# Layer 3 of a four-layer convolution stack: shifts from 8 on computed on TensorE as four 32-column tiles

## The chip, the cores and the metric

The kernel runs on one core of one Trainium2 chip. The metric is the device time of one execution in microseconds (us), given as the median over several runs. A profile of one execution comes beside it; its times are counted from the first instruction of that execution.

## The reference

Four layers work on `x`, an image of 4 batches, 32 rows, 32 columns and 16 channels in fp32. Each adds to `x` a function of `x` after a group norm. Layers 0 to 2 mix pixels with large dense tensors; they are not touched here. Layer 3 is a two-dimensional causal convolution with a filter given by its transfer function, written in the reference with Fourier transforms:

```python
def _L3_conv_ref(x, h0, numerators, denumerator):
    a = jnp.pad(denumerator, ((0, 0), (0, 0), (1, 0), (1, 0)), constant_values=1.0)
    b = jnp.pad(numerators, ((0, 0), (0, 0), (0, 0), (1, 0), (1, 0)), constant_values=0.0)
    H_truncated = jnp.fft.rfft2(b, s=(l1, l2)) / jnp.fft.rfft2(a, s=(l1, l2))
    h_truncated = jnp.fft.irfft2(H_truncated, s=(l1, l2))
    H = jnp.fft.rfft2(h_truncated, s=(2 * l1, 2 * l2))
    H_full = h0 + H[0]
    X = jnp.fft.rfft2(x, s=(2 * l1, 2 * l2), axes=(-3, -2))
    Y = jnp.einsum('...hwi,ijhw->...hwj', X, H_full)
    return jnp.fft.irfft2(Y, s=(2 * l1, 2 * l2), axes=(-3, -2))[..., :l1, :l2, :]
...
x = x + _L3_conv_ref(_gn(x), L3_conv_h0, L3_conv_numerators, L3_conv_denumerator)
```

What counts for this case: an output pixel in column w takes input pixels of columns w, w-1, ..., 0 only. An input that lies d columns to the left meets the filter's column d. The number d is called the shift; it runs from 0 to 31, and an output column w has no work for a shift above w.

## The kernel before

Nearly all of the time goes to layers 0 to 2 (`conv_layer`, matmuls of L336 and the multiply-and-sum of L344). The filter of layer 3 (its impulse response) is worked out beside layer 0 and left in DRAM as `hd`. Layer 3 itself is the last stretch of the program, and nothing of any other layer stands beside it.

The group norm of layer 3 leaves its result in `y3`, with partitions (8 image rows x 16 channels), then four row groups `cc`, then 31 zero columns followed by the 32 image columns, then the batch. A slice of `y3` that begins at column 31-d is the image shifted by d to the right, with zeros where it runs out of the image. This slice is the stationary operand (`lhsT`) of a matmul: 32 columns x 4 batches = 128 output partitions. So output partition n holds column n/4 of the image, and each quarter of 32 partitions ("block" in the change) holds eight image columns.

The moving operand (`rhs`) comes from a Toeplitz tile `t`, which `load_toeplitz(k)` builds from `hd` for four shifts, 4k to 4k+3 (`TQ` is 4; k runs from 0 to 7). It is made of eight DMAs (L501), four issued on SP and four on ACT, one for each group of 16 partitions. Each DMA carries 160 KB in runs of 640 bytes, so one tile is 1.31 MB. The pool `tp` holds three such tiles. The first three are loaded during layer 2 (`toeplitz`, stepped by `conv_layer`). The load of tile k+2 is written in the program at the beginning of step k, and it goes to the buffer that step k-1 has read; SP and ACT wait for TensorE's semaphore before they issue it.

The program is written with a manual schedule: each engine runs its instructions in the order in which they are written.

The loop over k, q and cc issues 8 x 4 x 4 = 128 matmuls at L564, all into one PSUM bank `po`. The width of a matmul's output falls with cc (16 channels x 32, 24, 16 and 8 rows: 512, 384, 256 and 128 columns). The trace has two matmul records and two weight loads for each fp32 matmul. After the loop VectorE adds `po` to `xo` (L571; `xo` is `x` transposed, L553), and SP stores `xo` (L572).

Of the kernel before, what the change touches and what calls it, by code (L numbers as in the profile page):

```python
# [32 lines left out]
ALU = mybir.AluOpType  # L33
# [4 lines left out]
P = 128  # L38
B, C, S = 4, 16, 32
# [8 lines left out]
PITCH = 40  # L48
HLEN = 8 + S * PITCH
TQ = 4  # L50
# [3 lines left out]
def conv_stack_kernel(ctx, tc, x, M, W, G, den, num, h0, cst, dft, one, idp, idq, out):  # L54
    nc = tc.nc
# [14 lines left out]
    def pair_psum():  # L70
        return ps.tile([P, 2, 512], F32, tag="pt", name="pt")

    def small_psum():
        return pair_psum()[:, 0, :]
# [420 lines left out]
    def load_toeplitz(k):  # L495

        t = tp.tile([P, C, TQ * PITCH], F32, tag="t", name="t")
        hv = hd.rearrange("(j i) t -> i j t", j=C)
        for p in range(8):
            at = 8 + k * TQ * PITCH - p  # L500
            (nc.sync, nc.scalar)[p % 2].dma_start(  # L501
                out=t[p * C : (p + 1) * C], in_=hv[:, :, at : at + TQ * PITCH]
            )
        return t
# [17 lines left out]
    y3 = const.tile([P, 4, 31 + S, B], F32, name="y3")  # L522
# [11 lines left out]
    tp = ctx.enter_context(tc.tile_pool(name="tp", bufs=3))  # L534
    ts = []

    def toeplitz():
        for k in range(3):
            ts.append(load_toeplitz(k))
            yield  # L540

    xs = conv_layer(2, xs, norm3, toeplitz())
    drain()

# [7 lines left out]
    xo = work.tile([P, S, C], F32, tag="xo", name="xo")  # L552
    nc.scalar.copy(xo, px.rearrange("n (r j) -> n r j", j=C))  # L553

    po = small_psum()
    pov = po.rearrange("n (j r) -> n j r", j=C)
    for k in range(S // TQ):
        if k and k + 2 < S // TQ:
            ts.append(load_toeplitz(k + 2))
        t = ts[k]  # L560
        for q in range(TQ):
            dq = k * TQ + q
            for cc in range(4):
                nc.tensor.matmul(  # L564
                    pov[:, :, 8 * cc :],
                    lhsT=y3[:, cc, 31 - dq : 31 - dq + S, :].rearrange("p q b -> p (q b)"),
                    rhs=t[:, :, q * PITCH : q * PITCH + S - 8 * cc],
                    start=(dq == 0 and cc == 0),
                    stop=(dq == S - 1 and cc == 3),
                )  # L570
    nc.vector.tensor_tensor(xo, xo, pov.rearrange("n j r -> n r j"), ALU.add)  # L571
    nc.sync.dma_start(out=out, in_=xo)  # L572


# [81 lines left out]
```

## Time and profile before

| | |
|---|---|
| median of 3 runs | 3216.66 us (3215.99 to 3217.17) |
| profiled execution | 3216.64 us, of which 3214.8 us lie between its first and last instruction |
| layer 3's matmuls (L564) | from 3140.5 to 3210.9 us |
| 5 loads of `t` after the first three | issued from 3150.5 to 3191.3 us |
| final add (L571), store (L572) | from 3211.0 us, 0.69 us; issued at 3211.7 us |

The profile names the engines PE (TensorE's matmuls), PEld (its weight loads), DVE (VectorE), ACT (ScalarE), POOL (GpSimd) and SP (SyncE). A name with a q behind it is that engine's instruction queue. A line such as `L564 PE MATMUL pt<-t,y 128*128 128x512 f32` is a group of instructions: the source line, the engine, the operation, the tile written and the tiles read, the part of the array in use (rows * columns), and the shape of the result. `PEclk` is the granted share of TensorE's full clock. `DMA share` is the mean busy share of the core's 16 DMA engines; it can exceed 1, since an engine can have two packets under way at once.

### The profile page before, as it was taken

How to read it: one execution, taken by the hardware profiler on the slowest of the kernel's cores; microseconds unless marked ns; L12 is line 12 of the kernel's file. 1: busy time of each engine (PE TensorE's matmuls, PEld its weight loads, DVE VectorE, ACT ScalarE, POOL GpSimd, SP SyncE). 2: the span in 40 equal slices, each digit the busy share in tenths (PEclk: the TensorE clock that was granted, in tenths of full speed). 3: DMA queues.
4: the chain of work that ended last, by engine and by line, in shares of the span. 5: the costliest groups of instructions: out<-in, count | busy, mean ns of one | idle time of the engine just before them, and what ended most of it. 6: DMA issues, size and time to landing. Idle time of an engine off the chain costs nothing.

```text
span 3214.8 us, 38408 instructions
## 1 busy us (share of the span) xinstructions
PE 3148.2 (98%) x15852; PEld 1678.7 (52%) x15852; DVE 2054.8 (64%) x3294; ACT 75.7 (2%) x98; POOL 171.9 (5%) x124
## 2 busy tenths in 40 slices
PE   6999999999999999999999999999989999999998
PEld 3545566666666544444544445454444444444445
DVE  4666765666666766666666666766656666666660
ACT  0000000000000000000000000000000000000000
POOL 0002310000000000000000000000000000000000
PEclk9999999999999999999999999999999999999999
DMA  6544344343333554333433343365473343333306
GB/s 148 156 115 116 88 109 94 86 103 88 88 98 90 107 154 118 99 89 88 99 96 86 86 105 87 80 143 144 99 127 89 98 99 89 87 99 92 86 1 85
DMA packets 106383, 322.18 MB, mean 100 GB/s; under 512 B 29214, under 2 KB 59360, under 8 KB 81632
## 3 DMA queue, kind: packets, MB, share of 16 engines
q1 hardware_dynamic: 68608, 302.69, 39.2%
q10 hardware_dynamic: 37600, 17.04, 3.4%
q8 instruction: 124, 2.03, 0.3%
q14 instruction: 51, 0.42, 0.1%
HBM read 313.01 MB, written 6.68 MB: 99 GB/s over the span
## 4 chain that ended last, share of the span: by engine, by line
PE 94%; DMA 4%; DVE 1%; ACTq 0%; issue 0%; SPq 0%; POOL 0%; ACT 0%; DVEq 0%; POOLq 0%
PE pt L336 90%; PE pt L564 2%; DMA t<-hd 1%; DMA img<-y 1%; DMA im<-img 1%; PE pt L199 1%; DMA td<-s 1%; DMA v<-td 0%; DMA fd<-ft 0%; DVE junk L344 0%; DMA h0s<-in_h_dram 0%; PE pt L470 0%; ACTq L223 0%; PE pt L387 0%; POOL hs L452 0%
## 5 line engine op out<-in xcount | busy, mean ns | idle before, releaser
L344 DVE SCALAR_TENSOR_TENSOR junk<-pt,w 128x1024 f32<-128x1024 f32 x1536 | 1880.8, 1224 | 1031.7 <-PE pt L336 1017.4
L336 PE MATMUL pt<-im,ga 64*128 64x512 f32 x6144 | 1834.4, 592 | 38.0 <-DMA im<-img 20.5
L336 PE MATMUL pt<-im,gb 64*128 64x512 f32 x6144 | 1824.4, 589 | 0.9 <-DMA im<-img 0.9
L336 PE MATMUL pt<-im,gn 64*128 64x512 f32 x3072 | 1487.7, 807 | 1.9 <-DMA im<-img 1.9
L336 PEld LDWEIGHTS pt<-im,gb 64*128 64x128 f32 x6144 | 706.5, 186 | 737.7 <-issue 705.0
L336 PEld LDWEIGHTS pt<-im,ga 64*128 64x128 f32 x6144 | 708.6, 188 | 422.8 <-DVE junk L344 246.6
L336 PEld LDWEIGHTS pt<-im,gn 64*128 64x128 f32 x3072 | 355.3, 186 | 295.4 <-issue 290.2
L266 POOL TENSOR_TENSOR ga<-ga,cs 128x1024 f32<-128x1024 f32 x48 | 113.4, 2362 | 2215.5 <-DMA ga<-in_G_dram 2153.5
L273 DVE TENSOR_TENSOR gn<-g,gn 32x1024 fp32r<-32x1024 f32 x96 | 118.0, 1229 | 34.3 <-ACT gn L270 32.3
L344 DVE DVE_READ_ACCUMULATOR junk<-pt,w 128x1 f32 x1536 | 127.3, 83 | 0.0
L270 ACT CAST gn<-g 128x1024 fp32r<-128x1024 f32 x48 | 50.2, 1047 | 2318.7 <-DMA g<-in_G_dram 2020.4
L564 PE MATMUL pt<-t,y 128*128 128x512 f32 (+3 forms) x256 | 70.4, 438 | 0.0
L564 PEld LDWEIGHTS pt<-t,y 128*128 128x128 f32 x256 | 44.2, 193 | 26.2 <-issue 16.2
L571 DVE TENSOR_TENSOR xo<-xo,pt 128x512 f32<-128x512 f32 x1 | 0.7, 689 | 70.8 <-PE pt L564 70.8
L199 PE MATMUL pt<-mt,yt 128*64 128x512 f32 x96 | 21.9, 598 | 0.0
L231 POOL TENSOR_TENSOR xr<-x,xf 128x512 f32<-128x512 f32 x3 | 3.8, 1271 | 294.5 <-DMA xf<-fd 294.5
L470 PE MATMUL pt<-v,inv 64*128 64x512 f32 x16 | 8.6, 656 | 7.5 <-DMA v<-td 7.5
L199 PEld LDWEIGHTS pt<-mt,yt 128*64 128x64 f32 x96 | 6.4, 136 | 13.7 <-issue 9.4
L147 POOL COPY e<-y 32x612 f32<-32x612 f32 x6 | 4.2, 693 | 171.7 <-DVE y L146 171.7
L104 PE MATMUL pt<-s,cs 128*128 128x2 f32 x16 | 3.3, 276 | 9.7 <-DVE s L101 9.7
L408 POOL TENSOR_TENSOR H<-H,d 128x256 f32<-128x256 f32 (+1 forms) x10 | 8.2, 825 | 66.6 <-DVE d L413 66.3
L408 POOL TENSOR_TENSOR t<-s 128x256 f32<-128x256 f32 (+1 forms) x15 | 11.3, 754 | 0.0
(57 smaller groups left out, 141.0 us busy)
## 6 DMA issues: line engine op xcount, KB each, us to landing
w<-in_W_dram SPq DMA_DIRECT2D x192, 1024.0 KB
ga<-in_G_dram SPq DMA_DIRECT2D x96, 256.0 KB
gb<-in_G_dram SPq DMA_DIRECT2D x96, 256.0 KB
g<-in_G_dram SPq DMA_DIRECT2D x48, 512.0 KB
mt<-in_M_dram SPq DMA_DIRECT2D x24, 512.0 KB
t<-hd SPq DMA_DIRECT2D x32, 160.0 KB
t<-hd ACTq DMA_DIRECT2D x32, 160.0 KB
im<-img ACTq DMA_DIRECT2D x72, 67.5 KB
```

The lines of the kernel that those rows point to most:

```text
L104: nc.tensor.matmul(pm[:, :2], lhsT=avg, rhs=s, start=True, stop=True)
L147: nc.gpsimd.tensor_copy(ye[a][96:, :, :, 1:, :], ys[a][96:, :, :, :3, :])
L199: nc.tensor.matmul(pf[64 * h : 64 * h + 64], lhsT=yt[:, 4 * part + k].rearrange("k b c -> k (b c)"), rhs=mts[k][:, h, :], start=(k == 0), ...
L231: nc.gpsimd.tensor_tensor(xr, xt, xf, ALU.add)
L266: nc.gpsimd.tensor_tensor(gv, gv, mid.unsqueeze(1).to_broadcast([P, GC * 8, C]), ALU.subtract)
L270: nc.scalar.copy(gn, g9)
L273: nc.vector.tensor_tensor(lo, g9[r : r + 32], lo.bitcast(F32), ALU.subtract)
L336: nc.tensor.matmul(pt[:, half, :], lhsT=w[rows, blk % GC, :], rhs=im[rows, :, b % 2, :, :S], start=n == 0, stop=n == 2,)
L344: nc.vector.scalar_tensor_tensor(junk, pt.rearrange("p h m -> p (h m)"), 0.0, wt, ALU.min, ALU.mult, accum_out=acc[b // 2][:, b % 2, blk : ...
L408: mul = lambda o, u, w: nc.gpsimd.tensor_tensor(o, u, w, ALU.mult)
L470: nc.tensor.matmul(pq[:, h, :], lhsT=inv[two], rhs=v[two, bass.ts(part, 8)].rearrange("g p m -> g (p m)"), start=True, stop=True,)
L564: nc.tensor.matmul(pov[:, :, 8 * cc :], lhsT=y3[:, cc, 31 - dq : 31 - dq + S, :].rearrange("p q b -> p (q b)"), rhs=t[:, :, q * PITCH : q ...
```

## The change

Shifts 0 to 7 (k of 0 and 1) are computed as before. For shifts from 8 on, TensorE's array is used as four tiles of 128 rows x 32 columns. Each tile takes one quarter of the output (a block, eight image columns) and one shift of its own, with its own stationary and moving operand. Pairs of block and shift in which every stationary value is zero are left out: for shifts 8 to 15 three blocks are left, for 16 to 23 two, for 24 to 31 one. The list `slots` packs the pairs that remain in fours: 3 slots for each k of 2 and 3, 2 for 4 and 5, and 1 for 6 and 7. A slot is run for each of the four `cc`.

Where a block is computed in the tile of its own PSUM quarter, it adds to `po`. In the other cases the tile's quarter differs from the block's; the sum goes to another bank (`other`), and VectorE adds it to the right quarter of `xo` later (five adds of 32 partitions, L566). A second pair of PSUM banks is taken for that.

The order of the k is no longer 0 to 7 but 1, 7, 6, 5, 4, 3, 2, 0, and the loads follow this order. After the change the matmul is at L591, the final add at L606 and the store at L607.

In the built program the 128 matmuls become 32 matmuls of 128 output partitions and 192 of 32. The number and the size of the DMAs on SP and on ACT are the same, and so is all that stands ahead of layer 3 except for which k the first three loads take.

```diff
+    order = [1, 7, 6, 5, 4, 3, 2, 0]
+
     def toeplitz():
-        for k in range(3):
+        for k in order[:3]:
             ts.append(load_toeplitz(k))
             yield
...
-    po = small_psum()
-    pov = po.rearrange("n (j r) -> n j r", j=C)
-    for k in range(S // TQ):
-        if k and k + 2 < S // TQ:
-            ts.append(load_toeplitz(k + 2))
-        t = ts[k]
-        for q in range(TQ):
-            dq = k * TQ + q
+    banks = [pair_psum(), pair_psum()]
+    po, other = banks[0][:, 0], {1: banks[0][:, 1], 2: banks[1][:, 0], 3: banks[1][:, 1]}
+    def add(block, tile, bank):
+        out = xo[32 * block : 32 * block + 32]
+        src = bank[32 * tile : 32 * tile + 32].rearrange("n (j r) -> n r j", j=C)
+        nc.vector.tensor_tensor(out, out, src, ALU.add)
+
+    slots = [
+        [[(None, None, q)] for q in range(TQ)],
+        [[(0, i + 1, 3)] + [(t, t, i) for t in range(1, 4)] for i in range(3)],
+        [[(0, 2, 2 + i), (1, 3, 2 + i), (2, 2, i), (3, 3, i)] for i in range(2)],
+        [[(t, 3, t) for t in range(4)]],
+    ]
+    group = lambda tile, block: (tile, block) if tile != block else None
+    every = [group(*m[:2]) for k in order for slot in slots[k // 2] for _ in range(4) for m in slot]
+    done = 0
+    for n, k in enumerate(order):
+        if n and n + 2 < len(order):
+            ts.append(load_toeplitz(order[n + 2]))
+        for slot in slots[k // 2]:
             for cc in range(4):
-                nc.tensor.matmul(
-                    pov[:, :, 8 * cc :],
-                    lhsT=y3[:, cc, 31 - dq : 31 - dq + S, :].rearrange("p q b -> p (q b)"),
-                    rhs=t[:, :, q * PITCH : q * PITCH + S - 8 * cc],
-                    start=(dq == 0 and cc == 0),
-                    stop=(dq == S - 1 and cc == 3),
-                )
-    nc.vector.tensor_tensor(xo, xo, pov.rearrange("n j r -> n r j"), ALU.add)
+                for tile, block, q in slot:
+                    at = 31 - TQ * k - q
+                    if tile is None:
+                        bank, cols, width = po, slice(0, P), S
+                    else:
+                        bank = po if tile == block else other[block]
+                        cols, width = slice(32 * tile, 32 * tile + 32), 8
+                        at += 8 * block
+                    nc.tensor.matmul(
+                        bank[cols].rearrange("n (j r) -> n j r", j=C)[:, :, 8 * cc :],
+                        lhsT=y3[:, cc, at : at + width, :].rearrange("p q b -> p (q b)"),
+                        rhs=ts[n][:, :, q * PITCH : q * PITCH + S - 8 * cc],
+                        start=group(tile, block) not in every[:done],
+                        stop=group(tile, block) not in every[done + 1 :],
+                    )
+                    done += 1
+        if k == 6:
+            add(3, 2, other[3])
+        elif k == 4:
+            add(3, 1, other[3])
+        elif k == 2:
+            for block in range(1, 4):
+                add(block, 0, other[block])
+    nc.vector.tensor_tensor(xo, xo, po.rearrange("n (j r) -> n r j", j=C), ALU.add)
     nc.sync.dma_start(out=out, in_=xo)
```

## The prediction

> **What bounds the kernel now.** I read the page first, then the chain of waits for the last 75 us, then the groups of that stretch by shape, then its windows with the DMA share, and last the DMA queues. On the page TensorE is busy for 98% of the span, and layer 3's matmuls are 70.4 us of it:
>
> ```profile
> PE 3148.2 (98%) x15852; PEld 1678.7 (52%) x15852; DVE 2054.8 (64%) x3294; ACT 75.7 (2%) x98; POOL 171.9 (5%) x124
> L564 PE MATMUL pt<-t,y 128*128 128x512 f32 (+3 forms) x256 | 70.4, 438 | 0.0
> L571 DVE TENSOR_TENSOR xo<-xo,pt 128x512 f32<-128x512 f32 x1 | 0.7, 689 | 70.8 <-PE pt L564 70.8
> ```
>
> The chain of waits of the last stretch (start, length, what) says that these matmuls alone set the end; no wait stands between them:
>
> ```profile
> 3140.71 70.21 PE pt L564 x256
> 3210.92 0.03 issue
> 3210.95 0.02 DVEq L571
> 3210.97 0.04 issue
> 3211.01 0.69 DVE xo L571
> ```
>
> So a faster matmul loop ought to help one for one, until the next thing is late. What is next is seen in the windows, whose last two columns are DMA share and GB/s:
>
> ```profile
> 3140.00:3150.50 10.50, 10.50 (x37) 6.55 (x36) 0.23 (x1) 0.58 (x1) 0.00 (x0) 0.86 0.01 2
> 3150.50:3160.80 10.30, 10.30 (x38) 6.35 (x38) 0.00 (x0) 0.00 (x0) 0.00 (x0) 1.00 0.97 134
> 3160.80:3170.40 9.60, 9.60 (x38) 6.12 (x37) 0.00 (x0) 0.00 (x0) 0.00 (x0) 1.00 1.16 156
> 3170.40:3179.90 9.50, 9.50 (x36) 5.86 (x35) 0.00 (x0) 0.00 (x0) 0.00 (x0) 1.00 1.25 135
> 3179.90:3191.30 11.40, 11.40 (x45) 7.38 (x44) 0.00 (x0) 0.00 (x0) 0.00 (x0) 1.00 1.24 139
> 3191.30:3199.70 8.40, 8.40 (x32) 5.25 (x31) 0.00 (x0) 0.00 (x0) 0.00 (x0) 1.00 0.94 99
> 3199.70:3211.00 11.30, 11.21 (x43) 7.01 (x42) 0.00 (x0) 0.00 (x0) 0.00 (x0) 1.00 0.00 0
> ```
>
> I cut the windows where, by the trace's semaphore updates, the last DMA of each of the five late loads of `t` lands: 3160.83, 3170.41, 3179.93, 3191.25 and 3199.70. From the first load to the last the DMA engines have no free time. The DMA view of 3150 to 3200 us confirms it, in 40 slices and for both queues:
>
> ```profile
> DMA  0699999689999999999999999999999999999910
> q1 hardware_dynamic: 5440, 3.28, 56.0%
> q10 hardware_dynamic: 5440, 3.28, 53.8%
> t<-hd SPq DMA_DIRECT2D x20, 160.0 KB
> ```
>
> The stretch thus has two limits that nearly touch. The last step of matmuls (four shifts, 8.63 us) starts at about 3210.9 - 8.6 = 3202.3; its tile has landed at 3199.7. There are 2.6 us between the two.
>
> **What the skill says.** (1) "TensorEngine Tiling (Array Packing)", Key Properties: column tiles load weights and multiply independently of one another, and a change of the tiling mode drains the array. The trace agrees for two tiles: layer 0's first term uses 128*64 tiles with two moving operands,
>
> ```profile
> 180.47 3.65 PE L199 MATMUL pt<-mt,yt 128*64 128x512 f32 x16
> 3144.70 1.49 PEld L564 LDWEIGHTS pt<-t,y 128*128 128x128 f32 x7 [0.24 <-issue]
> 3146.86 1.49 PEld L564 LDWEIGHTS pt<-t,y 128*128 128x128 f32 x7 [0.24 <-issue]
> ```
>
> 16 records in 3.65 us. In layer 3 a record of this width follows the last one after 0.43 us, so one after another they would take 6.9. The two weight-load lines give the period of one shift (two records each of 512, 384, 256 and 128 columns): 2.16 us. (2) "TensorE: Matmul & The Clock Gate", Part 3, measured 2.38x for three column tiles and 10.6x for 16 tiles of 32x32. No run here shows four yet. (3) The same page, Part 1: an idle window of some 3.4 us halves TensorE's clock. The trace agrees: the granted clock is 0.50 from 3136.0 to 3142.9, after little work. (4) "Trainium Kernel Development and Optimization", Key Constraints: DMAs issued by SP and ACT share the same 16 engines. The trace agrees: 56.0% + 53.8% of them.
>
> **The change, part by part.**
>
> *Matmuls.* Before: 32 shifts x 2.16 = 69.1 us, and 1.3 us more for the half clock at the start. After: 8 full shifts, and 3+3+2+2+1+1 = 12 slots of four tiles. A slot has the widths of a shift. With four tiles side by side it costs 2.16 us, so 20 x 2.16 = 43.2 us: 25.9 us of matmul time go. The slot's price is the unknown. Below 2.16 it cannot go, since each tile streams its own 1280 columns twice. Above: 4.3 if only two tiles run at once, 8.6 if none do. A slot issues 64 records (32 matmuls, 32 loads) where a shift issued 16. The Clock Gate page, Part 1, has about 62 ns of sequencer time per matmul when its hardware decoder is off; if weight loads cost as much, that makes an estimated 64 x 62 = 4.0 us. I take 2.2 to 2.6.
>
> *Order and loads.* Step k=1 comes first and is an old full step, so the first buffer comes free when it did, at 3150.5. The five late loads are the same bytes in the same runs. Their buffers come free earlier: k=7 ends at 3152.7, k=6 at 3154.8. That removes waits for TensorE from SP and ACT, but the DMA engines were full already. So I let them land as before: the first at 3160.8, the others at a mean of (3199.70 - 3160.83)/4 = 9.72 us, the last one (k=0) at 3199.7. Their bounds: at the best window's 156 GB/s a load takes 8.4 us and the last one lands at 3194.4; at 10.2 us it lands at 3201.6.
>
> *Who waits for whom.* TensorE has k=5 at 3160.8 (2 slots, 4.3), k=4 at 3170.5, k=3 at 3180.3 (3 slots, 6.5), k=2 at 3190.0. Each is shorter than the 9.7 us between landings, so TensorE stands idle for 3 to 6 us before each. If the half clock comes back, half of the time up to the next warm window is lost, 1.2 to 1.7 us a step. Even then k=2 ends at 3190.0 + 6.5 + 1.7 = 3198.2, ahead of the last tile. The two changes of tiling mode lie in such gaps as well.
>
> *Last step.* k=0 is a full step of 8.63 us and can't start before 3199.7. With 0.2 us for the wait and the last result: 3199.7 + 8.63 + 0.2 = 3208.5, against 3210.9. That is -2.4 us, about the slack of 2.6. With the half clock at its start it would be up to 1.7 later (-0.7).
>
> *Adds.* Five VectorE adds of 32 partitions: at most 0.69 us each by the row of L571. Those after k=6 and k=4 lie in gaps. Of the three after k=2 the first is waited for by k=0's first matmul (built so: the bank shares a PSUM tile with `po`): 3198.2 + 0.8 = 3199.0, hidden by the last load with 0.7 us to spare. The others lie beside k=0's matmuls. The cover is gone if a slot costs more than 2.5 us; then they add about 0.9. The final add and the store are unchanged.
>
> *Second PSUM pair.* It takes a buffer last read by small VectorE work at 3135.9, before layer 3: nothing.
>
> Sum: the profiled execution (3214.8 us span, 1.84 us around it, 3216.64) and the median of the runs, 3216.66, are the same for this purpose: 3216.66 - 2.4 = 3214.3.
>
> **The rivals.** A measurement of this kernel can tell about 0.2% (6.4 us) from no change.
> - *Main, 0.70:* the loads set the end, 3214.3; 3212 to 3216.5 with the half clock and 0.4 us more or less a load.
> - *The loads go faster, 0.07:* the backlog on both queues lets every load run at 8.4 us. Last landing 3194.4, end 3203.2, time 3209.0. For it: the window with 156 GB/s. Against: the later windows hold a backlog too and have 135 and 139.
> - *Two tiles at a time, or issue-bound, 0.13:* slots of 4.0 to 4.3 us. Then k=5 ends at 3169.5, k=4 at 3179.0, k=3 at 3192.9, k=2 at 3205.8, k=0 at 3214.5 to 3215.4: 3.6 to 4.5 us late, 3220.3 to 3221.2. At 4.0 us a slot it is 2 to 3 us late.
> - *The other side, slower, 0.10:* the place is the slot. Loads hide it while it is short; from about 4.8 us on (75 ns a record: 3160.8 + 10 x 4.8 + 8.63 = 3217.4) the loss passes 6.4 us. With no overlap at all a slot costs 8.6: 3150.5 + 12 x 8.63 + 0.9 + 8.63 = 3263.6, 52.7 us late, 3269. For it: four moving streams at once from every partition are seen nowhere here, nor so many records a microsecond. Against: two streams ran without loss.
>
> **How the numbers follow.** The time is the main case's, 3214.3. The range, 3210.0 to 3221.0, holds the main case and nearly all of the third. The second and the fourth fall out, 0.17 together. Faster by over 0.2% (under 3210.2) is the second case, 0.07; slower by over 0.2% (over 3223.1) the fourth, 0.10; the same 0.83.
>
> **What would show it.** In the profile after: L591's records of four tiles starting within some tens of ns, 2.2 us a slot; TensorE's busy share in the last stretch far lower, with gaps ended by `DMA t<-hd`; DMA share still about 1 from 3151 to 3199; the chain going from the last `t<-hd` to 8.6 us of L591 to L606. I am wrong on the bound if TensorE has no gaps ahead of k=5 to k=2, on the loads if the last one lands before 3196, on the slot if its period is over 2.6 us.

## The result, and the profile after

The two kernels can't be told apart. The changed one took 3218.16 us (median of 6 runs, 3215.38 to 3219.32), the one before 3216.91 us (6 runs, 3214.52 to 3219.25); the ratio is 1.0003, with a 95% interval of 0.999 to 1.0015. A second comparison with more runs (e5) gave 0.9996 (0.9988 to 1.0004). The profiled execution took 3217.79 us, of which 3216.0 lie between its first and last instruction.

The four tiles do what they were meant to do. These are the groups of layer 3 on the page of the changed kernel (busy time, mean ns of one, idle time ahead and what ended it):

```profile
L591 PE MATMUL pt<-t,y 128*32 128x512 f32 (+4 forms) x448 | 53.5, 499 | 18.3 <-DMA t<-hd 17.9
L591 PEld LDWEIGHTS pt<-t,y 128*32 128x32 f32 (+1 forms) x448 | 27.1, 137 | 44.7 <-issue 38.2
L566 DVE TENSOR_TENSOR xo<-xo,pt 32x512 f32<-32x512 f32 x5 | 3.4, 682 | 57.8 <-PE pt L591 57.8
```

Matmul time fell from 70.4 to 53.5 us, and 17.9 us of idle time came, ended by `DMA t<-hd`. That group had no idle time before. Half clock took some 9 of the 53.5 us. This is an estimate from the trace's clock record: the matmuls ran at half clock for 3.5 us at the start, 5.8 in k=5, 5.6 in k=3 and 3.4 in k=0, and half of that is lost. The timeline of weight loads in k=7 and k=6 gives the price of a slot (start, length, group):

```profile
3151.23 0.13 PEld L591 LDWEIGHTS pt<-t,y 128*32 128x32 f32 x4 [0.30 <-issue]
...
3153.38 0.13 PEld L591 LDWEIGHTS pt<-t,y 128*32 128x32 f32 x4 [0.30 <-issue]
```

Four weight loads at a time, and 2.15 us from one slot to the next: just the period of one full shift. Each slot runs four matmul streams in the time of one.

The windows are cut at the first issue and at the landings of the late loads, as those of before were (length, PE busy, then the other engines, granted clock, DMA share, GB/s):

```profile
3140.00:3150.90 10.90, 10.90 (x39) 6.58 (x41) 0.01 (x1) 0.58 (x1) 0.00 (x0) 0.82 0.01 2
3150.90:3161.70 10.80, 4.39 (x64) 1.81 (x60) 0.69 (x1) 0.00 (x0) 0.00 (x0) 0.80 1.08 147
3161.70:3171.80 10.10, 7.37 (x64) 2.90 (x64) 0.00 (x0) 0.00 (x0) 0.00 (x0) 0.70 1.24 131
3171.80:3182.50 10.70, 4.51 (x64) 2.27 (x64) 0.68 (x1) 0.00 (x0) 0.00 (x0) 0.95 1.24 132
3182.50:3192.30 9.80, 9.40 (x96) 3.97 (x96) 0.00 (x0) 0.00 (x0) 0.00 (x0) 0.71 1.24 134
3192.30:3201.40 9.10, 6.67 (x96) 3.44 (x96) 2.04 (x3) 0.00 (x0) 0.00 (x0) 1.00 0.95 105
3201.40:3212.20 10.80, 10.56 (x32) 6.26 (x32) 0.02 (x1) 0.00 (x0) 0.00 (x0) 0.84 0.01 2
```

From 3150.9 to 3201.4 TensorE is busy for 4.4 to 9.4 us of each window and idle for the rest, while the DMA share stays at about 1 or above up to the last landing, at 3201.4. The DMA view of 3150 to 3205 us shows no opening:

```profile
DMA  0499999999999999999999999999999999991000
```

The end of the chain of waits has changed. Where one stretch of 70 us of matmuls stood, the loads now follow one another:

```profile
3152.29 9.41 DMA t<-hd
...
3161.72 10.04 DMA t<-hd
...
3171.78 10.74 DMA t<-hd
...
3182.55 9.79 DMA t<-hd
...
3192.36 9.02 DMA t<-hd
3201.38 0.20 issue
3201.57 10.58 PE pt L591 x32
3212.15 0.02 issue
3212.18 0.69 DVE xo L606
```

Five loads, then a full step of k=0, then the final add. The last step took 10.58 us; at full clock the same step took 8.88 (e10, below). The windows of its clock tell why:

```profile
3198.40:3201.80 3.40, 0.93 (x21) 0.57 (x10) 2.04 (x3) 0.00 (x0) 0.00 (x0) 1.00 0.34 38
3201.90:3205.20 3.30, 3.30 (x6) 1.69 (x5) 0.00 (x0) 0.00 (x0) 0.00 (x0) 0.50 0.02 5
3205.30:3212.00 6.70, 6.70 (x27) 4.26 (x25) 0.00 (x0) 0.00 (x0) 0.00 (x0) 1.00 0.00 0
```

TensorE waited for the last tile with only 0.93 us of work in one window, and was granted half of its clock (0.50) for the next.

### The profile page after: what moved, and what is told of

The parts are those of the page before. It is cut to its first block, busy times and chain, and to the rows that moved or that the text cites. A ratio compares the mean times of both kernels' runs of the same rounds, so it can differ in the third digit from the quotient of the medians.

```text
span 3216.0 us, 38799 instructions
## 1 busy us (share of the span) xinstructions
PE 3132.0 (97%) x16044; PEld 1682.7 (52%) x16044; DVE 2058.3 (64%) x3299; ACT 75.7 (2%) x98; POOL 171.8 (5%) x124
## 4 chain that ended last, share of the span: by engine, by line
PE 92%; DMA 6%; DVE 1%; ACTq 0%; issue 0%; SPq 0%; ACT 0%; DVEq 0%
PE pt L336 90%; DMA t<-hd 3%; DMA img<-y 1%; PE pt L591 1%; DMA im<-img 1%; PE pt L199 1%; DMA v<-td 0%; DMA inv<-in_idq_dram 0%; DMA fd<-ft 0%; DVE junk L344 0%; DMA td<-s 0%; PE pt L470 0%; PE pt L387 0%; PE pt L430 0%; ACTq L223 0%
## 5 line engine op out<-in xcount | busy, mean ns | idle before, releaser
L336 PEld LDWEIGHTS pt<-im,gb 64*128 64x128 f32 x6144 | 715.6, 186 | 730.6 <-issue 699.7
L336 PEld LDWEIGHTS pt<-im,ga 64*128 64x128 f32 x6144 | 718.1, 188 | 410.7 <-DVE junk L344 239.2
L591 PE MATMUL pt<-t,y 128*32 128x512 f32 (+4 forms) x448 | 53.5, 499 | 18.3 <-DMA t<-hd 17.9
L591 PEld LDWEIGHTS pt<-t,y 128*32 128x32 f32 (+1 forms) x448 | 27.1, 137 | 44.7 <-issue 38.2
L566 DVE TENSOR_TENSOR xo<-xo,pt 32x512 f32<-32x512 f32 x5 | 3.4, 682 | 57.8 <-PE pt L591 57.8
```

What stands on the lines that cost most here:

```text
L336: nc.tensor.matmul(pt[:, half, :], lhsT=w[rows, blk % GC, :], rhs=im[rows, :, b % 2, :, :S], start=n == 0, stop=n == 2,)
L566: nc.vector.tensor_tensor(out, out, src, ALU.add)
L591: nc.tensor.matmul(bank[cols].rearrange("n (j r) -> n j r", j=C)[:, :, 8 * cc :], lhsT=y3[:, cc, at : at + width, :].rearrange("p q b -> p ...
```

## The experiments

Two theories were set against each other. **Theory L**: before the change TensorE set the end; now the late loads of `t` do, so that the gain in matmul time lies in front of the landings. **Theory T**: TensorE still sets the end, and its own delays (half clock, changes of tiling mode, waits for the adds) eat the gain. Profiled executions begin layer 3 at different times (its transposes start anywhere from 3133.8 to 3143.2 us), so profiles are compared by the stretch from the start of the transposes (L549 or L551) to the start of the final add: 71.4 us before, 72.8 after.

### e1 and e2: both kernels without late loads

```diff
-            ts.append(load_toeplitz(order[n + 2]))
+            ts.append(ts[n - 1])
```

> The changed kernel without the five late loads of t: steps 4 to 8 read the tile that lies in their buffer from three steps earlier (so the filter columns of these five steps are not the right ones). Theory L (the late loads set the end after the change): nothing is left to wait for, so the matmul loop is 10.4 us for k=1 with the half clock, 12 slots of 2.15 = 25.9 and 8.6 for k=0, about 45 to 46 us instead of 71.7; the time falls by 25 to 26 us, to about 3192. Theory T (TensorE still sets the end: half clock, changes of tiling mode and waits for the adds eat what the tiles save): the time stays within 3 us of the changed kernel's 3218.

> The kernel before without its five late loads (the same part left out in the same way). Theory L: before the change TensorE set the end and every load landed at least 2.6 us ahead of its use, so the time stays at 3217, within 1.5 us. Theory T says the same. A fall by more than 3 us would mean that the loads cost something before the change too, by slowing the matmuls, say.

The changed kernel without its late loads took 3192.63 us, a ratio of 0.9919 (0.9904 to 0.9934) to the kernel before: 26 us less by the ratio, 23 by the medians. The kernel before without them took 3215.73 us, ratio 0.9997 (0.9989 to 1.0006); since not even that gained anything, neither a buffer nor another order of its loads could have helped it. So the loads cost the changed kernel all that the tiles save, and the kernel before nothing. The chain of e1 has no load in it:

```profile
3142.11 14.44 PE pt L591 x95
...
3156.65 0.70 DVE xo L566
...
3157.39 21.79 PE pt L591 x320
...
3179.20 0.69 DVE xo L566
...
3179.93 8.91 PE pt L591 x32
```

Ten slots in 21.79 us are again 2.15 to 2.2 each. Two adds now stand on the path, each with some 0.8 us of idle TensorE: the price that the prediction gave for the case that their cover is gone. The stretch is 47.9 us, 25 under the changed kernel's. The mode changes and the adds of Theory T are all still there, so they do not eat the gain. The half clock went together with the waits here; it is taken up with e7 and e12.

### e3 and e4: one buffer more

```diff
-    tp = ctx.enter_context(tc.tile_pool(name="tp", bufs=3))
+    tp = ctx.enter_context(tc.tile_pool(name="tp", bufs=4))
...
-        for k in order[:3]:
+        for k in order[:4]:
...
-        if n and n + 2 < len(order):
-            ts.append(load_toeplitz(order[n + 2]))
+        if n and n + 3 < len(order):
+            ts.append(load_toeplitz(order[n + 3]))
```

> The changed kernel with a fourth buffer for t and four loads ahead of layer 3 instead of three, so that four loads are late, not five. Theory L: one landing interval less, 9.9 us, so the last tile lands at about 3191.4 and the time falls by 9 to 12 us (the half clock of the last step may come or go by 1.7), to 3206 to 3209. Theory T: no change, 3218.

> The kernel before with the same fourth buffer and one late load less. Theory L: no change, 3217 within 1.5 us, since TensorE sets the end there. Theory T: no change either. A fall would show that the buffer helps whatever the matmuls are, and that e3 says nothing of the change.

With four buffers the changed kernel took 3210.37 us, ratio 0.9976 (0.9966 to 0.9987): by the ratio 7.7 us under the kernel before. The kernel before with four buffers had 1.0006 (0.9998 to 1.0015), no gain; its median, 3219.58, lay 1 us above the range that was expected. The profile of e3 has four late loads, a last landing 52.5 us after the transposes begin (62.0 in the changed kernel) and a stretch of 61.6 us: 11.2 less. The timed gain missed what was expected, 9 to 12 us and a time of 3206 to 3209: against the changed kernel's own ratio of 1.0003 it is 8.7 us, and the median is 3210.37. The sign and the pair of kernels say the same as e1 and e2.

### e5: the changed kernel again

> The changed kernel once more, for a second profile and a closer interval. From the start of layer 3's transposes to the start of the final add the profile of before takes 71.4 us and that of the changed kernel 72.8. Theory L: the late loads follow each other at 9.7 to 10.1 us whatever the run, and the last step is 8.8 us at full clock or 10.6 at half, as the clock's windows fall; so this stretch is 70.5 to 73 and the ratio within 0.1% of 1. Theory T: the stretch would follow TensorE's own delays, which are the same in every run, and stay at 72.8.

Ratio 0.9996 (0.9988 to 1.0004). Here the profile missed what was expected: the loads came at a mean of 10.61 us instead of 9.7 to 10.1, and the stretch was 75.9 us. The last step had the half clock again (10.57 us). That left the landings themselves to be explained (e7, e9 to e11), and the half clock (e12).

### e6: a short step last

```diff
-    order = [1, 7, 6, 5, 4, 3, 2, 0]
+    order = [1, 7, 0, 2, 3, 4, 5, 6]
...
-                        stop=group(tile, block) not in every[done + 1 :],
+                        stop=group(tile, block) not in [None, *every[done + 1 :]],
...
+    nc.tensor.matmul(po[:, :B], lhsT=ident, rhs=y3[:, 0, 0, :], start=False, stop=True)
```

(The closing matmul adds zeros and ends the sum in `po`, since the last step writes only one quarter of it. The adds are moved behind k=3, 5 and 6.)

> The changed kernel with only the order altered: 1, 7, 0, 2, 3, 4, 5, 6. The bytes, the buffers and the landings stay, but the step behind the last landing is k=6, one slot of 2.15 us, and not k=0, 8.6 us. Price: three adds of 0.7 us and a closing matmul of four columns, some 0.5 us, now stand behind it. Theory L: last landing 62 us after the transposes begin, then 2.4 to 4.3 + 0.5 + 2.1, so the final add starts at 67 to 69 us (72.8 in the changed kernel); the time is 3 to 6 us under the changed kernel's. Theory T: the sum of TensorE's work is the same, so with the adds the time is 2 to 3 us above it.

The chain behind the last landing:

```profile
3197.59 9.44 DMA t<-hd
3207.03 0.20 issue
3207.22 3.66 PE pt L591 x31
...
3210.91 0.69 DVE xo L566
...
3211.62 0.69 DVE xo L566
...
3212.34 0.70 DVE xo L566
...
3213.13 0.69 DVE xo L607
```

The final add starts 6.1 us after the last landing (10.8 in the changed kernel): the step became shorter by as much as was expected. But the last landing came 64.9 us after the transposes, not 62, so the stretch is 71.0 and not 67 to 69. It is 4.9 us under that of e5, whose loads took as long on the same chip. The timed ratio, 0.9997 (0.9988 to 1.0005), does not show it against e5's 0.9996; the 3 to 6 us that were expected of it did not come. The order alone is therefore not shown to help by the times; only the part behind the landing is seen to shrink.

### e7, e9, e10 and e11: what sets the landings

Two theories on the landings: they spread from run to run whatever the matmuls do (**Theory S**), or four-tile matmuls slow the loads (**Theory M**). e7 leaves out the matmuls of two of the four `cc` (640 of a slot's 1280 columns) in the steps of k=5 to k=2 (the list `every` is shortened to match); the loads, and all of k=1, 7, 6 and 0, stay. In e11 the slots of k=5 and k=4 run twice. e7 and e9 to e12 were each executed once, so it is their traces that are compared, not their times.

```diff
-            for cc in range(4):
+            for cc in (0, 3) if k in (5, 4, 3, 2) else range(4):
```

```diff
+        if k in (5, 4):
+            spare = small_psum()
+            again = [(slot, cc, m) for slot in slots[2] for cc in range(4) for m in slot]
+            for i, (slot, cc, (tile, block, q)) in enumerate(again):
...
```

> The changed kernel with half of the matmuls of k=5, 4, 3 and 2 left out (cc of 1 and 2), so that four row groups' sums lack these shifts. Loads, buffers and the last step stay. Theory L: TensorE's work in these steps costs nothing, so the stretch from the transposes to the final add stays at 70.5 to 73 us and the landings at 9.7 to 10.1 us. Theory T: 10 slots lose half of their matmuls (7 of 13 widths of the slot's 20 go, 10 x 1.08 us), so it is some 10 us shorter. If TensorE's reads of t slow the loads, the landings come at 9.2 us or less and it is 2 us shorter.

> The kernel before once more, for a second profile of its late loads. Open is why the loads of the changed kernel came at 9.92 and 10.61 us and not at the 9.72 of before. Theory S (the spread of the loads from run to run): the mean interval may be anything from 9.6 to 10.6. Theory M (four-tile matmuls slow the loads): 9.7 to 10.0, as in the two profiles with full matmuls so far.

> The changed kernel, for a third profile. Theory S: mean interval 9.6 to 10.6. Theory M: 9.9 to 10.6, and above that of e9 on the same chip.

> The changed kernel with the two slots of k=5 and of k=4 run a second time into a spare bank, 4.3 us of four-tile matmuls more in each of the first two intervals between landings; they still fit into them. Theory S: the first two intervals are as in e10, within 1 us together, and the stretch from the transposes to the final add is as in e10 within 3 us. Theory M: half of the matmuls of these steps left out (e7) went with 9.87 and 9.60, all of them with 10.06 and 10.76 or 11.01 and 11.73; twice the matmuls should give 11.5 or more each and a stretch 2 to 4 us longer.

Landings by the semaphore updates in the traces; the intervals are those between the five landings, the stretch runs from the transposes to the final add. e6 and e12 have five late loads too; e3, e4 and e8 have four and are left out.

| kernel | intervals, us | mean | last landing after the transposes | stretch |
|---|---|---|---|---|
| before | 9.58, 9.52, 11.32, 8.45 | 9.72 | 60.1 | 71.4 |
| e9, before again | 9.70, 9.75, 10.82, 9.07 | 9.83 | 61.7 | 71.9 |
| after | 10.06, 10.76, 9.81, 9.04 | 9.92 | 62.0 | 72.8 |
| e5, after again | 11.01, 11.73, 9.97, 9.72 | 10.61 | 65.1 | 75.9 |
| e10, after, third | 9.80, 10.52, 9.30, 8.49 | 9.53 | 60.2 | 69.3 |
| e6, short step last | 10.52, 12.20, 9.83, 9.46 | 10.50 | 64.9 | 71.0 |
| e7, half of the matmuls | 9.87, 9.60, 10.86, 8.22 | 9.64 | 60.5 | 71.3 |
| e11, k=5 and k=4 twice | 10.39, 10.55, 11.17, 7.56 | 9.92 | 61.9 | 72.5 |
| e12, with a filler | 11.17, 11.71, 10.96, 9.18 | 10.75 | 65.0 | 74.1 |

The three profiles of the changed kernel alone spread from 9.53 to 10.61: the same kernel differs from itself by more than its mean differs from that of before. Twice the matmuls in the first two intervals gave 20.9 us for both together, against 20.3 in e10 on the same chip, and not the 23 or more that Theory M asked for. So the landings spread from run to run, and four-tile matmuls are not shown to slow them. But the three slow profiles (e5, e6, e12) are all of four-tile kernels with all of their matmuls, and the kernel before has only two here, so a slowing of some tenths of a us a load can't be excluded. Where the spread comes from was not found. The trace's DMA records narrow it: in each of these traces the late loads are 10240 packets of 640 bytes, which took 96 to 97 ns each on average in the three slow profiles and 84 to 90 in the others, while the DMA share over the loads was 1.10 to 1.15 in all. So the packets took longer; no pause of the DMA engines is seen.

Half of the matmuls of four steps can be left out (e7) without a shorter stretch, as Theory L says; Theory T asked for some 10 us less, so it is out for these steps, half clock and all. e11 shows where this ends. Its last tile landed at 3195.68, but k=2, in part at half clock, took 8.39 us, and the last step waited for it and for the add behind it:

```profile
3188.21 8.39 PE pt L591 x96
...
3196.62 0.69 DVE xo L566
...
3197.36 8.91 PE pt L591 x32
```

That is 1.5 us behind the landing: here TensorE's own delay counted, since the last interval was short (7.56 us).

### e12: the clock of the last step

```diff
+            spare = small_psum()
+            for cc in range(4):
+                nc.tensor.matmul(
+                    spare.rearrange("n (j r) -> n j r", j=C)[:, :, 8 * cc :],
+                    lhsT=y3[:, cc, 31 : 31 + S, :].rearrange("p q b -> p (q b)"),
+                    rhs=ts[n][:, :, : S - 8 * cc],
...
```

> The changed kernel with one more shift's four matmuls (2.2 us, into a spare bank) between k=2 and k=0, in the gap ahead of the last landing. If the half clock is what makes the last step 10.6 us and not 8.8, it is 8.8 to 9.0 here, and the final add starts 9.2 us after the last landing and not 10.8. If the change of the tiling mode or the first wait for eight loads makes it, the last step stays at 10.6.

Its chain:

```profile
3195.05 6.67 PE pt L591 x96
3201.71 2.35 PE pt L608 x8
3204.07 0.26 issue
3204.32 8.88 PE pt L591 x32
3213.21 0.02 issue
3213.23 0.69 DVE xo L615
```

With work in the gap the last step took 8.88 us, and the final add started 9.1 us after the landing. By itself this does not show that the filler did it: the filler also takes over the change of tiling mode, which now lies ahead of it and not of the last step. What separates the causes are e10 and e3, which have no filler. There the change of mode and the wait for the eight loads stand directly ahead of the last step, and it took 8.88 us at full clock. In e10 (windows as above):

```profile
3194.80:3198.20 3.40, 1.78 (x5) 1.06 (x6) 1.79 (x3) 0.00 (x0) 0.00 (x0) 1.00 0.05 10
3198.20:3201.60 3.40, 3.40 (x14) 2.16 (x13) 0.00 (x0) 0.00 (x0) 0.00 (x0) 1.00 0.00 0
```

So the half clock explains the 10.6 us of the profile after, of e5 and of e7. When it comes can be read from the traces' clock records. The granted clock changes only at multiples of 3.41 us, so the stretch can be cut into windows of that length and TensorE's busy share counted in each. In layer 3, over all 14 profiles, every window at full clock with a busy share of 0.39 or less was followed by half clock, and every one with 0.41 or more by full clock. At half clock, 0.75 or less kept it and 0.76 or more ended it. The last window ahead of the last step had a share of 0.28 in the profile after, 0.11 in e5 and 0.33 in e7, against 0.53 in e10 and 0.63 in e3. In e12 it is 1.00, but k=2 alone would have given it about 0.4, right at the edge, so whether the filler was needed in that execution stays open.

### e8: what the theory asks for, all at once

Four buffers; the order 7, 1, 0, 5, 2, 3, 4, 6, so that the first buffer comes free early and one slot stands behind the last landing; the first matmul of k=1 ahead of k=7, so that all of `po` is begun; the closing matmul of e6. Each add follows the last matmul of its sum.

```diff
-    order = [1, 7, 6, 5, 4, 3, 2, 0]
+    order = [7, 1, 0, 5, 2, 3, 4, 6]
...
+    jobs = [(k, cc, *m) for k in order for slot in slots[k // 2] for cc in range(4) for m in slot]
+    jobs.insert(0, jobs.pop([k for k, *_ in jobs].index(1)))
...
+        if k not in steps[done + 1 :]:
+            if len(ts) < len(order):
+                ts.append(load_toeplitz(order[len(ts)]))
```

> All that Theory L asks for: a fourth buffer for t, the order 7, 1, 0, 5, 2, 3, 4, 6 (only the first matmul of k=1 goes ahead of k=7, so that all of po is begun), so that the first buffer comes free after some 6 us and not 11.5, and one slot behind the last landing. Theory L: first late load issued 6 us after the transposes begin, landing at 17, three more at 9.9 to 10.2 each, last at 47, then 2.4 to 4.3 + 0.5 + 2.1: the final add starts at 52 to 54 us, the time is 17 to 19 us under the kernel before, 3197 to 3199. Theory T: at or above the changed kernel's time.

3197.32 us, ratio 0.9936 (0.9923 to 0.995) to the kernel before: a gain of 0.64%, about 19 us by the medians, and clear of the changed kernel run beside it (e5). The final add was expected 52 to 54 us after the transposes and came after 50.9. The windows from the first late load's issue over its four landings:

```profile
3147.00:3157.60 10.60, 10.60 (x41) 6.70 (x40) 0.00 (x0) 0.00 (x0) 0.00 (x0) 1.00 1.09 151
3157.60:3167.00 9.40, 9.40 (x75) 5.22 (x77) 0.00 (x0) 0.00 (x0) 0.00 (x0) 1.00 1.24 138
3167.00:3177.50 10.50, 10.50 (x161) 4.87 (x157) 0.00 (x0) 0.00 (x0) 0.00 (x0) 1.00 1.24 136
3177.50:3186.70 9.20, 9.03 (x123) 5.05 (x114) 1.06 (x2) 0.00 (x0) 0.00 (x0) 1.00 0.97 104
```

PE is busy for nearly all of each window and the DMA share is about 1 in the same windows: both limits are met at once. No wait of TensorE for a load of `t` is left in this trace, and the clock is full in all four windows. The final add starts 20.5 us earlier than before.

## Why the prediction was right, and where its sum was off

The measured 3218.16 us lies inside the stated range, but above the 3212 to 3216.5 of the main case; the second comparison, e5, has 3215.39. The two limits were read rightly, and that is why the time hardly moved. The sizes of some terms were off, and they nearly cancelled the small gain.

- *What bounds the stretch:* right. The prediction read two limits that nearly touch, with 2.6 us between the landing of the last tile and its use, and said that no more than about that could be gained. e1 and e2 show both sides: the loads cost the changed kernel 23 to 26 us and the one before nothing.
- *The slot:* right, and at the floor: 2.15 us measured, against 2.16 as the floor and 2.2 to 2.6 taken. That takes away the two-tile, the issue-bound and the no-overlap rivals. A slot's 64 records came at 34 ns each, where the 16 of a shift before had come at 135. The claim of "TensorEngine Tiling (Array Packing)", Key Properties, that column tiles work independently holds for four tiles here: four streams ran in the time of one. "TensorE: Matmul & The Clock Gate", Part 3, has 2.38x for three.
- *The loads:* right in kind, off in size. The step "I let them land as before" put the last landing at 3199.7; it came at 3201.38, 1.7 us later (0.4 of it from a k=1 that ended later, the rest in the loads). The allowance of 0.4 us a load was too small: the changed kernel's mean ran from 9.53 to 10.61.
- *The gaps:* they came, but what the half clock does in them was mis-sized. TensorE waited 6.6, 2.6, 6.3, 0.4 and 2.5 us ahead of the five steps. The prediction allowed 1.2 to 1.7 us a step for half clock; k=5 took 7.37 us where k=4 with as many slots took 4.51, and k=3 9.40 where k=2 took 6.67, so it was 2.7 to 2.9 us; e10's k=3, with 7.95, lost 1.3. In the profile after the next landing hid this; in e11 less than that, in k=2, came through to the end. That k=2 would begin with hardly a gap was not foreseen: k=3 at half clock had filled its window.
- *The changes of tiling mode:* not both lie in gaps, as was said. k=7 follows k=1 without one. The change cost about 0.1 us there: 0.20 us from the start of the last 128-column record to that of the first tile's, where such records otherwise follow at 0.11.
- *The last step:* the term that was mis-sized most. "Can't start before 3199.7 ... 8.63 us" was taken at full clock, with the half clock at its start as an upper end. In the profile after, in e5 and in e7 it did come, and the step took 10.6 us; in e10 and e3 it didn't, 8.9. Its price of 1.7 us was sized rightly; whether it came hung on how the gap fell into the clock's windows (e12), which the prediction could not know.
- *The adds:* 0.68 us each, hidden; all of the last three ended ahead of the last landing. Where the cover went (e1) they cost the 0.8 to 0.9 us that was said.
- *The sum:* -2.4 us forecast; in the profile the end of the matmuls came 3.6 us later than the forecast's 3208.5, 1.7 from the landing and 1.95 from the last step. Over three profiles the stretch was 69.3 to 75.9, around the 71.4 and 71.9 of before. The shortest, e10, had the last step at full clock and the fastest loads: 2.6 us under e9 on the same chip, about the forecast. The timed ratios, 1.0003 and 0.9996, hold both no change and -2.4 us (0.9993), so that small gain is neither shown nor refuted.
- *The rival with faster loads:* no profile of the changed kernel had it; the best mean was 9.53 us, not 8.4. The DMA view of before is not quite without an opening (two slices at 6 and 8 tenths around the first landing, none after), but closing it brought nothing that these runs show.

## What to carry to other kernels

When one engine is busy all through a stage, ask what would be late next and by how much before pricing a faster engine: here the DMA engines were full in the same windows, and the slack between a landing and its use was the most that a shorter matmul loop could give. Such a change pays once the second limit is moved with it; one more buffer and an order that frees the first buffer early and leaves the shortest step behind the last landing turned nothing into 0.64%. A step that must wait also risks the half clock, which costs again just where nothing hides it.

## What was not expected of the hardware

- Four fp32 column tiles of 128 rows x 32 columns, each with its own moving operand from all 128 partitions, ran with no loss (2.15 us a slot against 2.16 for one full shift), at 34 ns a record over whole steps.
- What costs the clock here is TensorE's busy share in a window of 3.41 us, not the length of a gap: 0.39 and less of a window at full clock was followed by half clock, 0.41 and more was not (layer 3, 14 profiles; busy time as the traces count it). A gap of 2.5 us that left 0.93 us of work in one window cost it; gaps of 2.7 us (e3) and 1.9 us (e10) ahead of the same step, which left 1.94 and 2.16, and 1.78 us in the windows that they touch, did not. Elsewhere in these programs, with other matmuls, windows of up to 0.61 were followed by half clock, so the edge is not one number for all work.
- Five equal loads, with a DMA share of about 1 or above, landed from 7.6 to 12.2 us apart in the same place of the program.
